# Half-column products in one turn, mean tokens before W_v W_out, f2's row read from PSUM: a graph attention and slice attention kernel

## Chip, cores, metric

One core of a Trainium2 chip. The metric is the device time of one execution in microseconds (us), the median of the runs named. All runs quoted here are of the fast state. A verdict compares fast runs of both kernels of the same rounds. At the 2% mark every kernel below counts as the same as the kernel before; the 95% intervals given with the ratios tell the smaller differences apart. e1 to e4 ran on one chip, e5 to e8 on a second, e9 and e10 on a third; the kernel before ran with each group, at 2724.41, 2725.32 and 2723.79 us.

## The reference, cut to what matters

```python
# x: (32, 512, 256), adj: (512, 512); one batch is one of the 32
def _gat(inp, adj_mask, W, a):
    h = inp @ W
    f1, f2 = h @ a[:F_, 0], h @ a[F_:, 0]
    e = leaky_relu(f1[:, :, None] + f2[:, None, :], 0.2)
    if adj_mask is not None: e = where(adj_mask > 0, e, -9e15)
    return elu(softmax(e, axis=2) @ h)
# graph part: relu mlp1 -> gat without mask (512 wide) -> relu mlp2 -> gat with mask (256 wide)
# slice attention (8 heads, 64 slices), on layernorm(x):
slice_weights = softmax((x_mid @ W_slice + b_slice) / temp)
slice_token = einsum('bhnc,bhng->bhgc', fx_mid, slice_weights) / (slice_norm + 1e-5)
q, k, v = slice_token @ W_q, slice_token @ W_k, slice_token @ W_v
attn = softmax(q @ k.T * SCALE)
out_slice = attn @ v                      # mean of the slices' tokens, through W_v
out_x = einsum('bhgc,bhng->bhnc', out_slice, slice_weights)
return out_x @ W_out + b_out              # W_v W_out is one matrix wvo here
```

## The kernel before

The kernel doesn't issue its instructions in the order in which they are written. A recorder keeps them, and a list scheduler with a time model of its own places them; each step of a batch has a turn (`TURNS`), batches follow a period apart, and the first and last three batches are shifted by `HEAD` and `TAIL`.

```python
TURNS = {"load": -182.4, "norm1": -141.0, "mlp1": -121.9, ..., "gg": 151.6, "out": 181.5}
PERIOD, SPARE = 88.0, 0.00
HEAD, TAIL = (-3.1, -0.9, -0.1), (-1.0, -1.3, -1.0)
...
    def start_of(op):          # when may this operation be placed?
        t = op.ready
        for log in op.logs:    # its tiles
            if log not in until:
                kept = self.KEPT if log.bufs > self.KEPT and op.age > oldest and log.psum else 0
                if len(slots[log.tag]) <= kept or turn[log.queue][0] is not log:
                    return None
```

`KEPT` is 1: an operation of a batch that isn't the oldest under way may not take the last free PSUM buffer of its kind. PSUM is the memory that TensorE's products and transposes are written to here, SBUF the one for the other tiles on the chip. There are five `mm` buffers for products, two `tr` buffers for transposes and one `sm`.

```python
    def mm_tile(shape): return psum.tile(shape, F32, tag="mm", name="mm", bufs=5)
    def tr_tile(shape): return psum.tile(shape, F32, tag="tr", name="tr", bufs=2)
    EDGES = (0, B - 1)
    def by_dma(what, b): return what in FLIPPED and b not in EDGES
```

Most transposes of activations go through HBM (VectorE flips 32x32 blocks, transfers do the rest). In the first and the last batch (`EDGES`) TensorE does them, into `tr` buffers. In the profiles, `h,pT` are the products of the attention without mask, `o1T,w` those of mlp2, `wh,o2T` of h2 (the input of the masked attention), `h,p2T` of the masked attention, `s1T,wfx` and `nrow,bfx` of the slices' tokens, `gg,wT` of the output, and `xnT,w` of the next batch's mlp1. The masked attention:

```python
        f2b = new("f2b", [P, N])
        pt = tr_tile([P, N])
        for j in range(NT):
            nc.tensor.transpose(pt[:, ts(j)], h[:, j, D + 1 : D + 2].to_broadcast([P, P]), ident)
        nc.scalar.copy(f2b, pt)
        ...
        for i in range(NT):
            e = new("e", [P, N], bufs=2)
            nc.vector.scalar_tensor_tensor(e, f2b, h[:, i, D : D + 1], mbias[:, i, :], ...)
            ...                                   # leaky relu, -max, exp
            if by_dma("e", b):
                flip(e, stage[:, :, ts(i, Q)])
                continue
            pt = tr_tile([P, NT, P])              # first and last batch
            for j in range(NT):
                nc.tensor.transpose(pt[:, j, :], e[:, ts(j)], ident)
            nc.scalar.copy(pT..., pt...)
```

Slices' tokens and their attention:

```python
        nc.step = "tokens"                        # half-column products: 64 output rows each
        pm = mm_tile([P, NP, G])
        for p in range(NP):
            for k in range(KD):
                for s in range(2):
                    nc.tensor.matmul(pm[ts(s, C), p, :]..., wfx[:, k, ts(2 * p + s, C)], s1T[...], ...)
        for s in range(2):
            nc.tensor.matmul(pm[ts(s, C)], bfx[:, ts(s, C)], nrow[:, s], start=False, stop=True)

        def diagonal(dst, src):
            nc.vector.tensor_copy(dst(0), src(0))
            nc.scalar.copy(dst(1), src(1))
        ...                                       # tok, tokbd, q, scores, attbd, ra
        nc.step = "vo"                            # vo = tokens W_v W_out + b, then attention times vo
        for p2 in range(NP // 2):
            pv = mm_tile([P, 2, D])
            for s in range(2): nc.tensor.matmul(pv[:, s, :], tokbd[:, p, :], wvo[:, p, :], ...)
            nc.vector.tensor_tensor(vo[:, ts(p2, 2), :], pv, bout..., op=OP.add)
        ...                                       # attbd transposed, attT copied by VectorE
        nc.step = "gg"
        ...   nc.tensor.matmul(pg[:, s, :], attT[:, p, :], vo[:, p, :], ...)
        ...   nc.scalar.activation(gg[:, p, :], pg[:, s, :], AF.Copy, scale=ra[:, p : p + 1])
```

## Time and profile before

| | kernel before |
|---|---|
| median of the first 3 runs (range) | 2728.61 us (2726.51 to 2730.74) |
| profiled span | 2725.3 us |
| TensorE busy, records | 2667.5 us (98%), 11965 |
| VectorE, ScalarE busy | 2057.3 us (75%), 1117.4 us (41%) |
| granted TensorE clock | 0.997 |

Busy TensorE time is not much to go by here: products overlap and their ends are modelled. What does carry is the start of a record less the start of the next. Where it exceeds what that shape takes in a dense stream (0.216 us for 257 columns), something lay between them. The prediction below shows such lines and how they are used.

### The profile page before, as it was taken

What the parts mean: (1) busy time and instruction counts of PE and PEld (TensorE: products, weight loads), DVE (VectorE), ACT (ScalarE), POOL (GpSimd) and SP (SyncE); (2) the same over time, 40 slices, a digit from 0 to 9 for tenths busy, and PEclk for the clock granted to TensorE, in tenths of its full rate; (3) what the DMA queues carried; (4) which work ended last, traced back from release to release, by engine and by line L of the source; (5) the groups of instructions that cost most, each with busy time, mean ns of one, the idle gap of its engine ahead of it and who ended that gap; (6) DMA issues with size and microseconds to landing.
All of it is one profiled execution on the core that took longest, in us unless ns stands there. A gap on an engine that the chain in (4) does not pass through costs nothing.

```text
span 2725.3 us, 34426 instructions
## 1 busy us (share of the span) xinstructions
PE 2667.5 (98%) x11965; PEld 1988.7 (73%) x11965; DVE 2057.3 (75%) x5126; ACT 1117.4 (41%) x2102; POOL 124.6 (5%) x233
## 2 busy tenths in 40 slices
PE   7999999999999999999999999999999999999997
PEld 5777777777777777777777777777777777777765
DVE  6577777887777877778877778777788777787775
ACT  3443344443444443444434444334444334444332
POOL 1000000000000000000000000000000000000000
PEclk9999999999999999999999999999999999999998
DMA  5226555645555555556454555555565555564521
GB/s 167 58 57 165 135 140 143 168 133 154 139 148 139 148 154 139 138 145 165 133 153 130 158 139 145 157 140 141 147 161 134 158 137 145 140 156 137 133 78 53
DMA packets 465077, 375.35 MB, mean 138 GB/s; under 512 B 86532, under 2 KB 382088, under 8 KB 464904
## 3 DMA queue, kind: packets, MB, share of 16 engines
q1 hardware_dynamic: 461568, 371.01, 51.2%
q10 hardware_dynamic: 3336, 2.14, 0.3%
q8 instruction: 95, 1.56, 0.2%
q14 instruction: 78, 0.64, 0.1%
HBM read 197.96 MB, written 175.11 MB: 137 GB/s over the span
## 4 chain that ended last, share of the span: by engine, by line
PE 73%; DMA 13%; DVE 9%; SPq 2%; issue 2%; ACT 1%; ACTq 0%; POOL 0%; DVEq 0%; POOLq 0%
PE mm L255 70%; DMA o1T<-scr 4%; DMA scr<-s_stage 3%; SPq L255 2%; PE tr L255 2%; DMA s1T<-scr 2%; DVE u L255 1%; DMA w_raw<-scr 1%; DVE u_stage L255 1%; DVE xn L255 1%; DMA scr<-u_stage 1%; DVE xn_stage L255 1%; PE sm L255 1%; DVE vo L255 1%; DVE o1T L255 0%
## 5 line engine op out<-in xcount | busy, mean ns | idle before, releaser
L255 PE MATMUL mm<-wfc,o0T 128*128 128x257 f32 x2048 | 486.1, 379 | 0.0
L255 PEld LDWEIGHTS mm<-wfc,o0T 128*128 128x128 f32 x2048 | 386.2, 189 | 131.1 <-issue 84.9
L255 PE MATMUL mm<-h,pT 128*128 128x257 f32 (+1 forms) x2048 | 467.3, 382 | 0.4 <-ACT u L255 0.2
L255 PEld LDWEIGHTS mm<-h,pT 128*128 128x128 f32 x2048 | 379.9, 189 | 63.1 <-ACT u L255 4.8
L255 DVE TENSOR_TENSOR x<-mm,x 128x512 f32<-128x512 f32 x64 | 44.2, 691 | 292.8 <-PE mm L255 292.8
L255 PE MATMUL mm<-xnT,w 128*128 128x512 f32 x512 | 249.3, 602 | 2.1 <-ACT xnT L255 1.8
L255 PE MATMUL mm<-weff,xn2T 128*128 128x512 f32 x512 | 251.3, 594 | 0.0
L255 PE MATMUL mm<-xn,w 128*128 128x257 f32 x1024 | 244.7, 382 | 4.8 <-DVE w L255 4.8
L255 PE MATMUL mm<-h,p2T 128*128 128x257 f32 x1024 | 242.0, 380 | 0.7 <-ACT p2T L255 0.7
L255 ACT COPY h<-mm 128x257 f32<-128x257 f32 (+1 forms) x384 | 142.2, 370 | 241.2 <-PE mm L255 237.2
L255 PE MATMUL mm<-o1T,w 128*128 128x512 f32 x512 | 227.8, 597 | 10.1 <-DVE o1T L255 9.9
L255 PE MATMUL mm<-gg,wT 128*128 128x256 f32 x1024 | 235.9, 379 | 0.0
L255 PEld LDWEIGHTS mm<-xn,w 128*128 128x128 f32 x1024 | 191.4, 190 | 36.4 <-ACT w L255 5.7
L255 PEld LDWEIGHTS mm<-gg,wT 128*128 128x128 f32 x1024 | 189.6, 190 | 35.1 <-issue 6.5
L255 PEld LDWEIGHTS mm<-h,p2T 128*128 128x128 f32 x1024 | 187.0, 190 | 28.2 <-ACT p2T L255 0.9
L255 PEld LDWEIGHTS mm<-o1T,w 128*128 128x128 f32 x512 | 94.9, 190 | 126.3 <-issue 91.1
L255 DVE STREAM_TRANSPOSE o_stage<-o2T 128x512 f32<-128x512 f32 x64 | 45.6, 712 | 171.0 <-ACT o2T L255 171.0
L255 ACT ACTIVATE e<-e,nmax 128x512 f32<-128x512 f32 x128 | 92.5, 723 | 199.6 <-DVE nmax L255 199.4
L255 ACT ACTIVATE m<-m 128x512 f32<-128x512 f32 x192 | 120.3, 627 | 131.0 <-DVE m L255 130.9
L255 PEld LDWEIGHTS mm<-xnT,w 128*128 128x128 f32 x512 | 92.6, 191 | 68.8 <-issue 50.9
L255 ACT ACTIVATE m<-m,neg 128x512 f32<-128x512 f32 x192 | 138.0, 719 | 3.6
L255 DVE SCALAR_TENSOR_TENSOR u<-m,u 128x512 f32<-128x512 f32 x192 | 131.6, 686 | 9.1 <-ACT m L255 7.7
(144 smaller groups left out, 3917.7 us busy)
## 6 DMA issues: line engine op xcount, KB each, us to landing
scr<-xn_stage SPq DMA_DIRECT2D x240, 128.0 KB, 2.7
scr<-u_stage SPq DMA_DIRECT2D x120, 256.0 KB, 4.3
o1T<-scr SPq DMA_DIRECT2D x30, 1024.0 KB, 6.0
scr<-e_stage SPq DMA_DIRECT2D x120, 256.0 KB, 4.2
p2T<-scr SPq DMA_DIRECT2D x30, 1024.0 KB, 5.4
scr<-w_stage SPq DMA_DIRECT2D x120, 256.0 KB, 4.2
w_raw<-scr SPq DMA_DIRECT2D x30, 1024.0 KB, 6.7
xt<-in_x_dram SPq DMA_DIRECT2D x32, 512.0 KB, 4.6
```

Of the source, the lines that this page charges most:

```text
L255: getattr(getattr(self.nc, op.engine), op.method)(*op.args, **op.kwargs)
```

## The change

The intent: the half-column products of a batch are to come in one visit (an unbroken run of them), as TensorE pays for each change to and from them (0.31 us a visit by the prediction's reading of the trace); four products of 256 columns become four of 64; and one copy and one SBUF tile go. The scheduler's model learns of the price (`SWITCH`), and the turns and shifts are set anew.

```diff
-    "load": -182.4, "norm1": -141.0, "mlp1": -121.9, ..., "gg": 151.6, "out": 181.5,
+    "load": -128.7, "norm1": -94.4, "mlp1": -94.4, ..., "gg": 209.6, "out": 212.5,
-PERIOD, SPARE = 88.0, 0.00
+PERIOD, SPARE = 89.4, 0.00
-HEAD, TAIL = (-3.1, -0.9, -0.1), (-1.0, -1.3, -1.0)
+HEAD, TAIL = (-5.9, -0.7, -1.7), (2.7, -1.5, 154.2)
...
+            costs = [0.0 if op.joint else cost for op, cost in zip(ops, costs)]   # one key for all
...
-        f2b = new("f2b", [P, N])
-        pt = tr_tile([P, N])
+        f2b = tr_tile([P, N])
         for j in range(NT):
-            nc.tensor.transpose(pt[:, ts(j)], ...)
-        nc.scalar.copy(f2b, pt)
+            nc.tensor.transpose(f2b[:, ts(j)], ...)
...
-        nc.vector.tensor_copy(attT, pt)
+        attT = new("attT", [P, NP, G])
+        diagonal(lambda s: attT[ts(s, G), :, :], lambda s: pt[ts(s, G), :, ts(s, G)])
+        pa = mm_tile([P, NP, G])
+        for p in range(NP):
+            nc.tensor.matmul(pa[:, p, :], tokg[:, p, :], attT[:, p, :], start=True, stop=True)
+        diagonal(lambda s: meanbd[ts(s, C), :, ts(s, G)], lambda s: pa[ts(s, C), :, :])
...
-                nc.tensor.matmul(pg[:, s, :], attT[:, p, :], vo[:, p, :], start=True, stop=True)
+                nc.tensor.matmul(pg[:, s, :], meanbd[:, p, :], wvo[:, p, :], start=True, stop=True)
-                nc.scalar.activation(gg[:, p, :], pg[:, s, :], AF.Copy, scale=ra[:, p : p + 1])
+                nc.vector.scalar_tensor_tensor(
+                    gg[:, p, :], pg[:, s, :], ra[:, p : p + 1], bout, op0=OP.mult, op1=OP.add)
```

Cut: the transposes of tokbd into tokg and its copy by ScalarE, which replace vo; the accounting of `SWITCH` in the scheduler's model; a memset.

## The prediction

> **What bounds the kernel now.** I read the page first: busy shares, then the chain of waits.
>
> ```profile
> PE 2667.5 (98%) x11965; PEld 1988.7 (73%) x11965; DVE 2057.3 (75%) x5126; ACT 1117.4 (41%) x2102; POOL 124.6 (5%) x233
> ...
> PE 73%; DMA 13%; DVE 9%; SPq 2%; issue 2%; ACT 1%; ACTq 0%; POOL 0%; DVEq 0%; POOLq 0%
> ```
>
> TensorE is busy 98% of the span, all over it, at a full granted clock. Busy matmuls overlap and their ends are modelled, so 98% does not say whether the array is fed back to back. So I took the timeline of TensorE over one middle batch (1400 to 1490 us) and used start to start times: the start of a group less the start of the next, over the count. 18 products of 257 columns take 3.90 us, 0.216 each; 512 columns 0.429; a 128 wide transpose 0.109. Priced like that (64 row outputs at 0.038, the four bias products at 0.107), the 11965 records come to about 2608 us. The rest of 2725.3 is 8.1 us before the first transpose, 4.3 after the last product and some 105 of gaps. Of the gaps 12 lie in the first 100 us, some 24 in the last 125, and 67 in the steady part, 2.3 per batch of 83.4 us. So there are two ways to gain: less work on TensorE, and fewer gaps between its instructions. Time saved on other engines counts only where it ends such a gap.
>
> Columns: start, length, engine, operation, count, idle before it and what ended that.
>
> ```profile
> 1427.15 9.25 PE L255 MATMUL mm<-h,pT 128*128 128x257 f32 x42
> 1436.96 0.30 PE L255 MATMUL mm<-s1T,wfx 128*64 128x64 f32 x2 [0.56 <-DMA s1T<-scr]
> 1437.19 3.66 PE L255 MATMUL mm<-h,pT 128*128 128x256 f32 x14
> 1440.78 0.69 PE L255 MATMUL mm<-s1T,wfx 128*64 128x64 f32 x16
> 1441.40 2.00 PE L255 MATMUL mm<-h,pT 128*128 128x256 f32 x8
> 1443.32 0.68 PE L255 MATMUL mm<-s1T,wfx 128*64 128x64 f32 x14
> 1443.93 0.65 PE L255 MATMUL mm<-nrow,bfx 4*64 4x256 f32 x4
> 1444.62 1.10 PE L255 MATMUL mm<-xnT,w 128*128 128x512 f32 x2
> 1445.55 0.59 PE L255 MATMUL mm<-tok,wqk 128*128 128x256 f32 x2
> 1445.98 1.02 PE L255 MATMUL mm<-xnT,w 128*128 128x512 f32 x2
> 1446.84 1.46 PE L255 MATMUL mm<-wvo,tokbd 128*128 128x256 f32 x6
> 1448.14 1.00 PE L255 MATMUL sm<-tok,qbd 128*128 128x64 f32 x8
> 1448.98 0.65 PE L255 MATMUL mm<-wvo,tokbd 128*128 128x256 f32 x2
> ...
> 1456.78 5.78 PE L255 MATMUL mm<-gg,wT 128*128 128x256 f32 x26
> 1462.67 7.13 PE L255 MATMUL mm<-o1T,w 128*128 128x512 f32 x16
> ```
>
> The reader is to see that the half-column products (128*64) come in three visits, cut apart by the h,pT products, and that each visit costs more than its own work. The eight h,pT products between two visits take 1443.32 - 1441.40 = 1.92 us, and 8 x 0.216 is 1.73. Looked at record by record, the last full product before a visit takes 0.308 instead of 0.216 (+0.09), the last half product 0.152 instead of 0.038 (+0.11), and the second full product after it 0.104 more: **0.31 us a visit**. I count 88 visits in 32 batches. The first visit also stands too early: s1T has not landed (0.56 idle here, some 8 us in all in the steady part, and once 8.5 us near the end). And o1T,w waits, 0.28 us here and 0.5 on average, for the last transfer of o1T.
>
> **What the Trainium skill says.** "TensorEngine Tiling (Array Packing)", Key Properties, says that changing the tiling mode, not just the tile, drains TensorE. The trace agrees: 0.308 against 0.216 going in. "TensorE: Matmul & The Clock Gate", LDWEIGHTS, puts a weight load at the number of weight columns over 1.2 GHz, 107 ns for 128. So a product with only 64 moving columns should not get below that, and the trace has 0.84 us for eight such (sm<-tok,qbd), 0.105 each. I use this for the new mean-token products. "VectorE: DVE Perf Modes", Why PSUM operands drop a tier, says fp32 with a PSUM operand runs at 1x; two-operand fp32 work has no more in SBUF either. The trace agrees: vo<-mm,bout from PSUM takes 671 ns at 128x512, w<-w,mx from SBUF 682. So reading f2's row from PSUM should leave the 743 ns of e<-f2b,h,mbias alone.
>
> **The change part by part.** The built order of the new kernel was compared with the old, engine by engine.
>
> (1) Half-column products in one turn. In the built order all 16 (32 records) and the bias products follow the last h,pT product: one visit a batch. 88 - 32 = 56 visits go, at 0.31: **-17 us**. Between the end of the sums and s1T's first use there are now the whole of pv2 and pv, some 21 us of TensorE work, where before it was about 17; s1T lands some 16 to 17 us after the sums. The steady DMA waits before it go: **-8 us**. In the last but one batch the wait of 8.5 us should shrink too, as o1T,w products now stand ahead of it; I put that with the end, below.
>
> (2) Mean tokens first, W_v W_out last. vo goes: 4 products of 256 columns, 8 records x 0.217 = 1.73 us. Added are 4 transposes of tokbd (4 x 0.109 = 0.44) and 4 products of 64 columns (0.84). gg keeps four products with other operands. Net -0.45 us a batch, x32 = **-14 us** of TensorE.
> VectorE loses two vo adds (2 x 0.67) and the whole attT copy (0.66), and gets half an attT copy and half a meanbd copy (2 x 0.41) and four gg operations, estimated at 0.46 from u<-mm,rd (475 ns) and s<-mm,rn (462 ns), both 256 wide with a pointer from PSUM: +0.7 us a batch. ScalarE loses four gg (4 x 0.47) and f2b (0.59) and gets tokg (0.58, as f2b) and two halves (2 x 0.37): -1.1 us. VectorE goes from 75% to about 76%, still beside TensorE.
> But the path is longer by one turn: attbd, transpose, attT, mean tokens, meanbd, gg, where vo was computed aside before. What fills the turns is mlp1 of the next batch, 8 products of 0.858 us (two records each). Before the mean tokens stands one of these after the transposes, 0.86 us. VectorE's part needs drain (about 0.2) plus 0.41 after ra's reduction; ScalarE does tokg (0.58) and an o0T (0.69) before its 0.37 of attT. By my count attT is ready 0.1 to 0.3 us late. The last gg operations on VectorE run 0.43 to 0.46 apart, as fast as gg,wT (0.43 each) uses them up, with no filler between: 0.1 at most. In all 0.25 x 30 = **+8 us** of new waits.
>
> (3) f2's row from PSUM. TensorE's work is the same. The copy (0.59 us) leaves the path from h2 to e, where VectorE waits for f2b for 19 us in all, but TensorE has work then (only 0.8 us of its gaps are before products with p2T): **0 us**. The tile holds one of two transposing PSUM buffers some 10 us longer; in the steady batches no other transpose is near, in the two edge batches the transposes of e must share the one left, perhaps +1 us.
>
> (4) The turns moved. o1T,w now comes 18.7 us of TensorE work after the end of pv; before it was needed at 19.1 and ready at 19.3. But only its first product stands there, and four gg,wT follow: its 0.5 us a batch should stay or shrink a little: 0. At the end, the last batch is now held back behind the one before it, so that it runs e to out almost alone, with waits for softmax and layernorm, some 20 us by my count against 24 before: **-4 us**. The head is the same for its first half: 0.
>
> Sum: -17 - 8 - 14 + 8 - 4 = -35 us, so 2728.6 becomes **2694 us**, ratio 0.987.
>
> **The rivals.** First, VectorE or ScalarE binds in the pv part. TensorE no longer pauses between pv groups for token products, so PSUM buffers (five) must be emptied at its full pace while VectorE does pv2's leftovers, layernorm, u and its flips. Already before, TensorE waited here for u in most batches (0.19 and 0.26 us). If VectorE lags 0.5 to 1 us a batch, 15 to 30 us come back: 2710 to 2725. For it: both engines are well loaded there, and the built order puts two u evacuations late on VectorE. Against it: ScalarE is at 41% and VectorE has idle time after attT (6.75 us).
> Second, the longer attention path really stalls, 0.8 us a batch in place of 0.25: +17, 2711. For it: the small filler, and VectorE's single file. Against it: every turn has some filler.
> Third, the retuned order removes nearly all steady gaps, o1T's too, and much of the end: another -25, 2669. For it: gaps are 105 us in all, so there is room. Against it: o1T's transfer chain is unchanged.
> Fourth, the gain of (1) is hidden because TensorE would wait for o1T later anyway: then the 17 us come back at o1T,w: 2711.
>
> **Range and chances.** The TensorE work of (2) and the visits of (1) are counted, -31, and I trust them to a third. The waits are the uncertain part, +30 to -25. The range is **2670 to 2719**. Two per cent faster means below about 2675: chance 0.13. Within 2%: 0.85. Slower by over 2% needs a broken schedule: 0.02.
>
> **What would show it.** In the new profile: 32 visits of half-column products, so one 0.308 step a batch; no DMA wait before s1T in the steady part; TensorE's records 11965 + 32 x (4 + 8 - 8) = 12093; VectorE's busy time up by some 20 us, ScalarE's down by 35; e<-tr,h,mbias at about 743 ns; gg at 0.46 us on VectorE; a period near 82.4 us. The prediction is wrong if TensorE waits for u in pv or for attT, meanbd or gg by more than 0.5 us a batch, if o1T,w waits over 1 us, or if the last 125 us hold gaps far from 20 us.

## The result, and the profile after

The changed kernel takes 2735.99 us (median of 4 runs, 2733.37 to 2737.89) against 2729.68 for the kernel before (4 runs). The ratio is 1.0022 with a 95% interval of 1.0004 to 1.0039. A ratio is the mean time of one kernel's fast runs over that of the other's of the same rounds, so it isn't quite the ratio of the medians. The change costs some 6 us where a gain of 35 was predicted, and the time lies outside the predicted range.

The page after, busy shares:

```profile
PE 2659.7 (97%) x12093; PEld 1977.8 (72%) x12093; DVE 2086.1 (76%) x5222; ACT 1091.6 (40%) x2038; POOL 132.3 (5%) x234
```

12093 records, as counted ahead; VectorE's busy time is up by 29 us (20 predicted), ScalarE's down by 26 (35 predicted). There are 34 visits, where 32 were predicted and the kernel before has 88. `e<-tr,h,mbias`, which now reads f2's row from PSUM, takes 743 ns, as it did from SBUF. The timeline of TensorE over the same part of a batch:

```profile
1427.23 1.15 PE L262 MATMUL mm<-s1T,wfx 128*64 128x64 f32 x32
1428.32 0.65 PE L262 MATMUL mm<-nrow,bfx 4*64 4x256 f32 x4
1428.89 1.98 PE L262 MATMUL mm<-xnT,w 128*128 128x512 f32 x4
...
1435.91 0.60 PE L262 MATMUL tr<-ident,attbd 128*128 128x128 f32 x4
1436.35 1.02 PE L262 MATMUL mm<-xnT,w 128*128 128x512 f32 x2
1437.42 1.10 PE L262 MATMUL mm<-attT,tokg 128*128 128x64 f32 x8
1438.36 1.08 PE L262 MATMUL mm<-xnT,w 128*128 128x512 f32 x2
1439.43 1.99 PE L262 MATMUL mm<-wvo,meanbd 128*128 128x256 f32 x8
```

All 32 half-column records of this batch stand in one visit, with no wait for s1T ahead of it. From xnT,w to attT,tokg there are 1.07 us for two records worth 0.858, and from the next xnT,w to wvo,meanbd again 1.07: two new waits of 0.2 us, plus the slower product after each. From batch 6 to batch 26, by the start of the first h2 product (wh,o2T), the period fell from 83.10 to **81.82 us**. I priced every record of these 20 batches as in the prediction and put what was left between records to the record that came late, in us per batch:

| | before | after |
|---|---|---|
| records at their dense pace | 80.84 | 80.44 |
| into, within and out of half-column visits | 0.67 | 0.11 |
| before h,pT (first products after a visit; u) | 0.33 | 0.00 |
| before s1T,wfx (transfer) | 0.32 | 0.00 |
| before o1T,w (transfer, add) | 0.62 | 0.20 |
| before attT,tokg and wvo,meanbd | 0.00 | 0.53 |
| before xnT,w (transfer xnT; first products after a visit) | 0.10 | 0.42 |
| the rest | 0.22 | 0.12 |
| period | 83.10 | 81.82 |

So the steady gain is there. It was lost elsewhere. The span cut at the start of h2 of batches 6, 26 and 29, in us, with the experiments beside it (spans of the profiled runs):

| | to 6 | 6 to 26 | 26 to 29 | 29 to end | out products of batch 30 to those of 31 |
|---|---|---|---|---|---|
| before | 552.9 | 1661.9 | 249.5 | 261.0 | 30.3 |
| after | 555.7 | 1636.4 | 251.7 | 287.8 | 73.6 |
| e1 shift only | 558.5 | 1635.9 | 251.9 | 305.4 | 73.4 |
| e2 buffer only | 554.2 | 1635.5 | 251.7 | 288.5 | 74.4 |
| e3 both | 554.0 | 1638.8 | 245.5 | 269.0 | 32.9 |
| e4 before, last f2 in PSUM | 553.9 | 1660.3 | 248.8 | 291.0 | 68.1 |
| e5 shifts alone | 554.7 | 1642.8 | 245.8 | 305.7 | 74.5 |
| e6 f2 in a product buffer | 555.0 | 1635.9 | 245.1 | 270.7 | 37.3 |
| e8 ends tuned | 552.6 | 1636.4 | 245.4 | 259.0 | 36.4 |

The 25.5 us won in the middle are given back in the last stretch, 26.8, with 5 more at the head and before the end. The last stretch by engine, of each kernel (columns: stretch; its length; busy time and records of TensorE, weight loads, VectorE, ScalarE, GpSimd; granted clock; DMA share; GB/s). Before, then after:

```profile
2464.30:2725.30 261.00, 239.90 (x1147) 181.62 (x1145) 187.79 (x445) 95.86 (x182) 10.36 (x19) 0.97 0.37 99
```

```profile
2443.80:2731.50 287.70, 249.12 (x1147) 184.06 (x1145) 189.43 (x453) 91.76 (x174) 8.65 (x19) 0.93 0.31 85
```

The same 1147 TensorE records take 27 us more: TensorE idles more, and the granted clock over the stretch is lower, 0.93 against 0.97. Where it idles, the timelines of the end show. Before:

```profile
2632.87 0.60 PE L255 MATMUL tr<-ident,e 128*128 128x128 f32 x4
...
2640.10 0.66 PE L255 MATMUL tr<-ident,e 128*128 128x128 f32 x4 [0.60 <-ACT e L255]
...
2683.56 7.07 PE L255 MATMUL mm<-gg,wT 128*128 128x256 f32 x32
```

After:

```profile
2646.17 7.17 PE L262 MATMUL mm<-gg,wT 128*128 128x256 f32 x32 [0.19 <-DVE gg L262]
2653.18 0.60 PE L262 MATMUL tr<-ident,e 128*128 128x128 f32 x4
2654.46 0.66 PE L262 MATMUL tr<-ident,e 128*128 128x128 f32 x4 [0.68 <-ACT p2T L262]
2657.58 0.66 PE L262 MATMUL tr<-ident,e 128*128 128x128 f32 x4 [2.47 <-ACT e L262]
...
2661.32 9.43 PE L262 MATMUL mm<-h,p2T 128*128 128x257 f32 x32 [0.68 <-ACT p2T L262]
2679.35 1.94 PE L262 MATMUL tr<-ident,xn 128*128 128x128 f32 x8 [8.59 <-DVE xn L262]
```

The gg,wT lines are batch 30's out products; tr<-ident,e are the last batch's (31). Before, e of batch 31 was transposed 50 us ahead of batch 30's out products, and the two batches filled each other's waits. After, it starts at 2653.18, at the very moment that the last of batch 30's products is through. Batch 31 then runs alone, with 8.59 us of idle time for its layernorm, for one. Some of its products are slow as well: from 2659.0 to 2665.8 us, right after the waits shown, the granted clock is 0.50.

### The profile page after: what moved, and what is told of

It reads as the page before. It is cut to its first block, busy times and chain, and to the rows that moved or that the text cites. A ratio compares the mean times of both kernels' runs of the same rounds, so it can differ in the third digit from the quotient of the medians.

```text
span 2731.5 us, 34620 instructions
## 1 busy us (share of the span) xinstructions
PE 2659.7 (97%) x12093; PEld 1977.8 (72%) x12093; DVE 2086.1 (76%) x5222; ACT 1091.6 (40%) x2038; POOL 132.3 (5%) x234
## 4 chain that ended last, share of the span: by engine, by line
PE 79%; DVE 9%; DMA 5%; ACT 3%; issue 2%; SPq 1%; POOL 0%; ACTq 0%; DVEq 0%; POOLq 0%
PE mm L262 76%; PE tr L262 2%; PE sm L262 1%; DMA xnT<-scr 1%; DVE w L262 1%; DVE u L262 1%; SPq L262 1%; DMA scr<-xn_stage 1%; DMA scr<-s_stage 1%; DVE e L262 1%; ACT attbd L262 1%; DMA o1T<-scr 1%; ACT o0T L262 1%; ACT tokg L262 1%; ACT m L262 0%
## 5 line engine op out<-in xcount | busy, mean ns | idle before, releaser
L262 PE MATMUL mm<-h,pT 128*128 128x256 f32 (+1 forms) x2048 | 457.3, 379 | 2.7 <-DVE pT L262 2.7
L262 PE MATMUL mm<-xnT,w 128*128 128x512 f32 x512 | 259.2, 614 | 5.9 <-DMA xnT<-scr 3.5
L262 PE MATMUL mm<-xn,w 128*128 128x257 f32 x1024 | 245.5, 382 | 11.7 <-DVE w L262 8.7
L262 PEld LDWEIGHTS mm<-gg,wT 128*128 128x128 f32 x1024 | 189.8, 190 | 43.8 <-issue 12.7
L262 DVE SCALAR_TENSOR_TENSOR e<-tr,h,mbias 128x512 f32<-128x512 f32 x128 | 92.4, 743 | 73.5 <-PE tr L262 73.5
L262 ACT ACTIVATE u<-mm,rd 128x256 f32<-128x256 f32 x192 | 89.8, 469 | 140.1 <-DVE rd L262 61.2
```

The lines of the kernel that those rows point to most:

```text
L262: getattr(getattr(self.nc, op.engine), op.method)(*op.args, **op.kwargs)
```

## The experiments

Two theories of the lost end. **BUFFER**: f2's row of the last batch, now held in one of the two `tr` buffers, blocks the transposes of e, as `KEPT` reserves the other buffer for batch 30. Of e there are only two SBUF buffers, so its third block can't be made before the first has been transposed; the row is thus not given up either, until batch 30 is done. **SHIFT**: it is the new shift of 154.2 that holds the last batch back.

### e1_shift_only and e2_buffer_only

```diff
-HEAD, TAIL = (-5.9, -0.7, -1.7), (2.7, -1.5, 154.2)
+HEAD, TAIL = (-5.9, -0.7, -1.7), (2.7, -1.5, -1.0)        # e1
```

> The changed kernel with one number undone: the last batch's shift 154.2 back to -1.0. Two theories of the lost end. BUFFER: the last batch (no transfers, so its e is transposed by TensorE) keeps f2's row in one of the two transposing PSUM buffers, and the recorder keeps the other free for the older batch, so the transposes of e cannot be placed before the batch before it is done. Then undoing the shift does not help: the 16 transposes of e still follow the last out products (gg,wT) of batch 30, as they already do in the built order; out products of the last two batches start 62 to 75 us apart (73.5 in the changed kernel, 30.3 in the kernel before), time 2736 to 2760 us. SHIFT: the hold-back itself serialises the last batch; then the distance falls to 30 to 40 us and the time to 2695 to 2710.

```diff
-        f2b = tr_tile([P, N])
+        f2b = pt = tr_tile([P, N])                         # e2; shift 154.2 kept
...
+        if b == B - 1:
+            f2b = new("f2b", [P, N], tag="stage")
+            nc.scalar.copy(f2b, pt)
```

> The changed kernel, with f2's row of the last batch alone copied to SBUF again (into the stage buffer, which the last batch doesn't use), shift 154.2 kept. BUFFER: it is necessary but the shift was chosen for the blocked end and still holds the last batch back, so the built order of the end is the same as before this edit: time within 5 us of the changed kernel (2731 to 2741). If the copy alone gave it all: 2700.

e1 took 2753.13 us (ratio to the kernel before 1.011, 1.0096 to 1.0125), e2 2733.76 (1.004, 1.0024 to 1.0055). Undoing the shift made it worse, by 17.6 us in the last stretch, and left batch 31's out products 73.4 us behind: SHIFT alone is out. Giving the buffer free with the shift in place changed nothing either, as expected. As long as the end is blocked, holding the last batch back is the better order: it makes the best of the blocked buffer, and isn't the cause.

### e3_buffer_and_shifts and e5_shifts_alone

```diff
-HEAD, TAIL = (-5.9, -0.7, -1.7), (2.7, -1.5, 154.2)
+HEAD, TAIL = (-2.3, 0.0, 0.0), (0.7, 0.7, 0.9)             # e5; e3 has e2's edit as well
```

> f2's row of the last batch in SBUF, and the shifts of the first and last batches set anew (head -2.3, 0, 0; tail 0.7, 0.7, 0.9). BUFFER: the transposes of e of the last batch stand among batch 30's w and sums products, out products of the last two batches 28 to 36 us apart, the steady gain of 1.26 us a batch survives to the end: 2700 to 2722 us, ratio to the kernel before 0.989 to 0.997. SHIFT alone predicts the same, so this run only shows how much of the loss lies at the end; if it stays above 2730, both are wrong.

> The shifts of e3_buffer_and_shifts in the changed kernel, but f2's row of the last batch still in a transposing PSUM buffer: one edit away from e3. BUFFER: the transposes of e wait for batch 30 to be done; out products of the last two batches 62 to 75 us apart, time 25 to 45 us over e3, 2733 to 2755. If e3's gain came from its shifts: within 5 us of e3 (2704 to 2714).

e3 took 2708.80 us (0.994, 0.9928 to 0.9952), e5 2744.76 (1.0073, 1.0056 to 1.009). The two are one edit apart, the copy of one row in one batch, and differ by 36 us, nearly all of it in the last stretch (269.0 against 305.7). They ran on different chips, but the kernel before took 2724.41 and 2725.32 us there.

### e4_before_f2last

The kernel before, with only the last batch's row read from PSUM.

```diff
-        f2b = new("f2b", [P, N])
         pt = tr_tile([P, N])
...
-        nc.scalar.copy(f2b, pt)
+        if b == B - 1:
+            f2b = pt
+        else:
+            f2b = new("f2b", [P, N])
+            nc.scalar.copy(f2b, pt)
```

> The kernel before, with a single edit: in the last batch alone f2's row is read from PSUM (no copy). All but the last batch is untouched, the shifts are its own. BUFFER: the transposes of e of the last batch move behind batch 30's out products, the out products of the last two batches part from 30.3 us to 60 to 70, time +22 to +40 us (2751 to 2770). SHIFT: there is no hold-back here, so no change: within 3 us of before.

It took 2756.78 us (1.0117, 1.0104 to 1.013). Four instructions' source and one copy of 0.59 us less cost 30.0 us in the last stretch, with no shift and none of the other parts of the change. In the timeline of TensorE in e4:

```profile
2661.24 1.98 PE L255 MATMUL mm<-s1T,wfx 128*64 128x64 f32 x32 [10.17 <-DMA s1T<-scr]
...
2674.62 7.07 PE L255 MATMUL mm<-gg,wT 128*128 128x256 f32 x32
2681.52 0.60 PE L255 MATMUL tr<-ident,e 128*128 128x128 f32 x4
```

The transposes of e moved from ahead of the out products to right behind them. The wait for batch 30's s1T was there before too (8.46 us); but in the other turns batch 31's work no longer fills in. From batch 30's first slice weights (weff,xn2T) to its out products TensorE is busy 26.14 of 44.90 us, where it was 40.35 of 52.40, and from there to the end it takes 79.50 us, where it took 41.80.

### e6_f2_other_buffer

Is it the reading from PSUM, or the buffer that is held? e3's shifts, no copy, but the last batch's row in one of the five product buffers:

```diff
-        f2b = tr_tile([P, N])
+        f2b = (mm_tile if b == B - 1 else tr_tile)([P, N])
```

> The shifts of e3, f2's row of the last batch read from PSUM by VectorE, as in the change, but in one of the five matmul buffers rather than one of the two for transposes; no copy. If the cost is the held transposing buffer: as e3, 2702 to 2715, out products of the last two batches 30 to 38 us apart. If reading the row from PSUM is itself the cost: as e5, 2733 to 2755.

2708.73 us (0.9947, 0.9932 to 0.9962), as e3. The timeline has the transposes of e ahead of the out products again:

```profile
2608.85 0.60 PE L262 MATMUL tr<-ident,e 128*128 128x128 f32 x4
...
2657.10 7.07 PE L262 MATMUL mm<-gg,wT 128*128 128x256 f32 x32
```

So here VectorE reads the last batch's row from PSUM at no cost that shows; what cost 36 us is which buffer held it. That the other `tr` buffer is refused by `KEPT`, and not only shared, is read from the scheduler's text and from where the transposes of e start in every blocked run, at the end of batch 30's out products; no run changed `KEPT` itself.

### e7_more_visits

The price of a visit by itself: e3 with eight of a batch's sixteen half-column products ordered between h,pT products again.

```diff
-                keys[op] = age * PERIOD + at + part / sum(costs) * (till - at)
+                keys[op] = age * PERIOD + at + part / sum(costs) * (till - at) - op.early
...
+            nc.early = (5.0, 3.0, 0.0, 0.0)[p]
```

Cut: e3's edits, and the line that sets `op.early`.

> e3 with its half-column products pulled apart again: eight of the sixteen products of a batch are ordered 5 and 3 us earlier, between h,pT products. 124 visits in the built order instead of 34, the other products in nearly the same order. At the 0.31 us a visit (0.09 going in, 0.11 coming out, 0.10 for the second product after) read in the kernel before, 90 more cost 28 us: 2730 to 2742, a steady period 0.8 to 1.0 us longer than e3's 81.94. If TensorE would have waited anyway at the next hand-over (attT, o1T), less than 10 us.

2751.38 us (1.0092, 1.0076 to 1.0109), 42.6 us over e3 where 28 were expected, and above the range given; e3 ran on another chip, and by the two ratios it is 41. The trace has 124 visits against 34, and the period is 83.44 against 81.94. The timeline of e7:

```profile
1529.83 0.45 PE L262 MATMUL mm<-s1T,wfx 128*64 128x64 f32 x8
1530.21 2.00 PE L262 MATMUL mm<-h,pT 128*128 128x256 f32 x8
1532.14 0.69 PE L262 MATMUL mm<-s1T,wfx 128*64 128x64 f32 x16
1532.76 0.64 PE L262 MATMUL mm<-nrow,bfx 4*64 4x256 f32 x2
1533.33 1.98 PE L262 MATMUL mm<-xnT,w 128*128 128x512 f32 x4
```

Record by record a visit costs 0.09 going in, 0.06 at the second half product, 0.11 coming out and 0.10 at the second full product after it: 0.37, where I had counted 0.31 and left the 0.06 out. The bias products (nrow,bfx), which the new order also parted, cost more: 0.09, 0.16, 0.20 and 0.10. Two plain visits and one of these make 1.29 us a batch of the 1.50 that the period grew; the rest is waits that came (0.26 before sm<-tok,qbd) and waits that went (xnT,w and o1T,w). The rival, that TensorE would have waited anyway (under 10 us), fails here: the visits were paid.

### e8_ends_tuned, and e10_e8_again

e6, with the last three batches' shifts set apart for the front (to o1), the middle (to pv2) and the back:

```diff
-HEAD, TAIL = (-2.3, 0.0, 0.0), (0.7, 0.7, 0.9)
+HEAD, TAIL = (-2.3, 0.0, 0.0), ((0.1, 0.7, 7.6), (0.3, 5.2, -21.3), (4.4, -9.4, -38.2))
...                                                         # cut: which shift goes to which step; e6's buffer
```

> e6 with the last three batches' shifts set apart for their front, middle and back steps. Both theories leave the steady part alone (81.9 us); the gap before the end should shrink by some 5 to 12 us more: 2696 to 2707 us, ratio to the kernel before 0.988 to 0.993. A miss is above e6's time.

> e8 again, on the same chip as e9, to compare with: 2690 to 2700 us, ratio to the kernel before 0.989.

e8 took 2694.95 us (0.989, 0.9874 to 0.9907), e10 2696.11 (0.9898, 0.9883 to 0.9913). Its last stretch, 259.0 us, is the first that isn't longer than the kernel before's, and the whole is at what was predicted for the change, 2694. That is no confirmation: the ends were tuned for it, and the terms are others than the predicted ones.

### e9_split_copies

Why TensorE waits twice as long as I had counted before the mean tokens and gg. `diagonal` copies one half by VectorE, the other by ScalarE. In the trace they never run side by side (in none of the 32 batches, for attT and meanbd alike): VectorE's half of meanbd is followed by ScalarE's, which has waited for it. From the timeline of all engines in the changed kernel:

```profile
1438.56 0.42 DVE L262 COPY meanbd<-mm 64x256 f32<-64x256 f32 x1 [1.60 <-PE mm L262]
1439.02 0.37 ACT L262 COPY meanbd<-mm 64x256 f32<-64x256 f32 x1 [1.65 <-DVE meanbd L262]
```

```diff
-        diagonal(lambda s: attT[ts(s, G), :, :], lambda s: pt[ts(s, G), :, ts(s, G)])
+        for c in (ts(0, 2), ts(1, 2)):
+            diagonal(lambda s: attT[ts(s, G), c, :], lambda s: pt[ts(s, G), c, ts(s, G)])
...                                                         # meanbd in the same way; on e8
```

> e8 with the half copies of attT and meanbd each cut in two by pair of heads (four copies of 64x128 in place of two of 64x256), the built order of TensorE in the steady part unchanged. Claim: the two halves of such a copy don't run side by side, ScalarE's waits for VectorE's (a semaphore in the built program; 0.42 then 0.37 us in the trace), so the turn is some 0.4 us longer than I counted in the prediction, and TensorE waits 0.27 us a batch before the mean tokens and 0.26 before gg. Cut in two, the first products can start after half of it: the wait before gg should go (0.26 to under 0.06), that before the mean tokens fall by about 0.1 only (an o0T of ScalarE stands in front of it), together 0.3 to 0.4 us a batch, 9 to 12 us: 2683 to 2690 us, period 81.5. If the waits come from elsewhere (longer sums of small copies, VectorE late), the time stays at e8's 2695 or grows.

2690.91 us (0.988, 0.9863 to 0.9896) against e10's 2696.11 on the same chip: 5 us rather than 9 to 12. The wait before gg went, as expected (0.26 to none). That before the mean tokens didn't fall: 0.33 against 0.27, now in two parts; what sets it stays open. The period is 81.85 against 81.97; e8 and e10, one kernel, differ by more (81.82, 81.97), so it isn't shown that the steady part gained at all. Some 0.1 of the 0.2 us that were saved a batch came back before o1T,w, whose products wait for a transfer (0.24 a batch against 0.14); xnT,w waits about as before, in this batch 1.45:

```profile
1426.48 2.54 PE L265 MATMUL mm<-xnT,w 128*128 128x512 f32 x4 [1.45 <-DMA xnT<-scr]
```

In the steady part TensorE now often waits for the transfers of xnT and o1T, so a shorter attention turn alone gains little. That is argued from the moved waits; no run took the transfers away. Of the 8.0 us between the profiled runs of e10 and e9, 2.2 lie between batches 6 and 26 and 3.6 in the last stretch (253.9 us against 257.5). e9 is the fastest kernel of the study.

## Why the prediction was wrong

**The steady part went as predicted, and rather better, partly by luck.** The visits were to give 17 us; their price was right in kind but under-counted (0.37 a visit, e7), so 54 fewer are worth some 20. The s1T waits (8) went, 0.32 a batch. TensorE's work fell by 0.40 us a batch, 12.7 in all, for 14 predicted; a 64-column product takes 0.112 rather than 0.105. New waits of the longer attention path were put at 8 us and are 0.53 a batch, 16, just over the 0.5 named as a sign of error: this term was mis-sized. Half of it is the wait for meanbd (0.26), which had no term of its own; I took the two half copies to run side by side, the trace has them one after the other, and with them cut in two (e9) this wait goes. The wait for attT (0.27) is at the upper end of what I gave it. Two terms that I put at 0 moved: o1T,w waits 0.42 less a batch, xnT,w 0.32 more. These three misses, of 8 to 13 us each, cancel in part. Together 1.28 us a batch (83.10 to 81.82) for about 1.0 predicted (83.4 to 82.4). The first rival (u in the pv part) did not come; the second (the attention path stalls 0.8 a batch) came in half; the third (o1T's wait shrinks) came in part; the fourth (the gain lost before o1T,w) did not come.

**The step that failed** is in part (3): "in the two edge batches the transposes of e must share the one left, perhaps +1 us". In the last batch they don't share it. The scheduler keeps the last free buffer for the older batch, so the last batch gets none, and it's serialised behind batch 30. (The first batch is itself the oldest; its transposes of e run, at 89 to 96 us.) e4 measures this step alone at +30 us, and e5 against e3 at 36. I had the rule in the kernel's text before me, and priced the held buffer as if only its time counted, not who may take the other one.

**Part (4) failed with it.** I read the shift of 154.2 as a harmless retuning and expected 4 us less at the end. It was 26.8 more. The count of "some 20 us" of waits in a batch that runs alone was too low: priced as above, the last 125 us hold 47.7 us of gaps and slow products, against 24.6 in the kernel before. Batch 31's layernorm alone left TensorE idle for 8.59 us, and the first ten of its p2T products took 0.43 us (the first 0.59) instead of 0.216, at a granted clock of 0.50. And the new shift was the sign: a last batch that must be held back by nearly two periods to get the best end is a batch that can't overlap.

What I named as a sign of error, "the last 125 us hold gaps far from 20 us", was the right place to look.

## What to carry to other kernels

A tile moved from SBUF to PSUM may cost no time by being read there (743 ns either way here), but it holds a buffer of a small pool; ask in every kind of iteration, the first and the last above all, who else needs that pool and by which rule it is handed out. When the steady gain of a change is right and the total isn't, cut the span at the same event of the same iterations in both traces: the stretch that lost shows at once. And pull apart what was joined (e7) to learn a price, rather than trust one reading of it.

## What the Trainium skill lacked or had wrong

- "TensorEngine Tiling (Array Packing)", Key Properties, names the drain on a change of tiling mode and gives no figure. Here a visit to half-column products costs 0.37 us in four places: 0.09, 0.06, 0.11 and 0.10, the last at the second product after the visit. 90 visits more, some of them around parted bias products, cost 42.6 us in all (e7).
- "PSUM — Partial Sum Buffer", Terms, says that different quadrants (32 partitions each) of one bank may be accessed at the same time. In this program it isn't done: VectorE and ScalarE copy partitions 0 to 63 and 64 to 127 of one PSUM tile, and one waits for the other, 0.42 then 0.37 us; in 30 of the 32 batches ScalarE's half of meanbd stood idle until VectorE's was done. The two engines' halves of u, which share an SBUF tile but come from two PSUM tiles, overlap in 81 of 192 cases. That points at the shared PSUM tile; no run separated it. No page says that two such readers of one PSUM tile are put in order.
- "TensorE: Matmul & The Clock Gate", LDWEIGHTS: its formula gives 107 ns for 128 weight columns, and products with 64 moving columns follow each other by 0.105 to 0.112 us here. That agrees; no run shows that the weight load is what sets this pace.
